# Operands asked for earlier and in smaller lots, a weight copy placed by product count, and the next image's norm spread over other steps, in a hand-ordered attention kernel

## The chip, the cores and the metric

The kernel runs on one core of a Trainium2 chip. The metric is device time in microseconds, the median of several runs. The core has the engines PE (TensorE, matmuls; PEld is its weight load), DVE (VectorE), ACT (ScalarE), POOL (GpSimd) and SP (SyncE, here only an issuer of DMAs).

## The reference

Two layers work on x, four images of 32 x 32 tokens with 768 channels, in float32. Each layer is a group norm (32 groups), an attention with 12 heads of 64 channels, decomposed relative positions in its scores, an output projection, and the addition to x.

```python
def attention(x, Wqkv, Wproj, Rh, Rw):             # x: (4, 32, 32, 768), normed
    q, k, v = split(x @ Wqkv)                      # 12 heads, S = 1024 tokens, 64 each
    bias = q . Rh (rows)[..., :, None] + q . Rw (columns)[..., None, :]
    attn = softmax(scale * q @ k.T + bias)         # 1024 x 1024 for each head
    return (attn @ v) @ Wproj                      # + bias of the projection

x = x + attention(group_norm(x), ...layer 0...)
x = x + attention(group_norm(x), ...layer 1...)    # with a bias on q, k and v
```

## The kernel before

**Pairs and steps.** Two layers of four images are eight passes, called images (`im`, 0 to 7). An image has six pairs of heads, so there are 48 pairs `g`; pair 0 of an image is the first, pair 5 the last. A pair takes eight steps `n`, of 128 query rows for both heads, 384 steps in all. The loop over `units` writes the order of the instructions of every engine by hand; nothing is reordered later. In a step it issues, among others, the position sums of two steps ahead (`biases`, L461 on POOL), the scores of the next step (`scores`: PE L475, DVE L484, ACT exp L488), a part of the work in `todo`, the transposes of this step (`turn`, DVE L515) and the division of the next (`divide`: DVE reciprocal L495, then POOL L499 for one head and ACT L501 for the other).

**The way of the probabilities.** DVE transposes 32 x 32 blocks into `tb`, two steps to a tile. At odd steps both tiles are written to DRAM (`td`, L518), and a few steps later read back in another order (`pt`, L526), for the product with v (`weigh`, PE L545; then the copy to `attn`, DVE L554 or L557). There are three `tb` buffers for two tiles in a quarter, so the second transpose of an even step waits until the last write of td has landed.

**Fill work.** `todo` is a list of generators: the projection of q and k of the next pair (`project_in`, PE L268), half a projection of v (`project_values`, PE L376, DVE L390 and L391), and four groups of the output projection (`project_out`, PE L621). `take(todo, n)` advances it by n products. `shares` says how many products a step takes, `first` how many of them are issued ahead of the transposes: in an ordinary pair [6, 9, 0, 6, 6, 6, 12, 0], the 12 in step 6 being the output groups.

**Projection of q and k.** Pairs 0 of each image and pair 1 are plain, with four units of six products. For the others, sums of weights and of inputs save three products: units of 6, 3, 6 and 6. (A pair g is called regular below when the pair after it, whose units it issues, is of this kind.) The sums of weights are made on POOL and ACT one pair earlier (`sum_weights`, L327 to L329), but for the last, which may only be made when unit 0 has read w0: DVE copies three blocks of w3 over the upper half of w0 (L336; the block A11 of the weights), POOL subtracts w3 from the lower half of w0 (L337). Unit 1 reads the copy, unit 2 what POOL wrote. Unit 0 is issued in step 0, units 1 and 2 in step 1. Then `positions` (PE L408, ACT L418) projects q on the position tables; its results go through DRAM (`tdr`) and come back as `rel` (SP L447).

**Output projection.** It is done in two parts p of three channel blocks each, with the partial sums kept in DRAM (`part`): part 0 of an image in its pairs 3 to 5, part 1 in the first three pairs of the next image. A group (o, i) has three matmuls of 128 x 512; then DVE adds the residual or the partial sum (L630 or L632) and the result is written back. `fetch` loads for four groups two tiles of weights (`wo`, pool of 2) and four of `res` (pool of 4, which the position tiles `t` and the tiles for the statistics of other images share), all in step 5, for groups in step 6.

**PSUM.** Of the tag "m" there are two buffers, which pj, pv, tp, av and o use in turn. So a fourth group needs that DVE is through with the second.

**DMA.** SP issues nearly all DMAs, in the order of the program. SP's and ACT's use eight semaphores in turn, so that an issue waits until the DMA eight places back has landed.

**The next image.** In pair 3 of an image the statistics of the next one are turned into means and scales (`stages`). In pair 4 its 12 tiles of x are loaded (`load_x`, three in each of steps 1 to 4) and normed in place (`apply`, DVE L228): tiles 0 and 1 in step 2, one in each of steps 3, 4 and 5, five in step 6, two in step 7.

The lists `early`, `later`, `mid`, `last`, `behind` and `behind2` hold issues that are put off: `early` runs at the start of a step, `later` becomes `early` in the next, `behind` runs after the scores.

## Time and profile before

| | us |
|---|---|
| median of 3 runs | 3700.49 (3692.12 to 3705.09) |
| profiled execution | 3706.17 |
| its span in the profile | 3704.4 |
| PE busy | 3465.2 (94%) |
| DVE busy | 2573.0 (69%) |
| POOL busy | 2495.1 (67%) |
| ACT busy | 1990.5 (54%) |
| matmuls of the projection of q and k (L268) | 958.5 |
| matmuls of the output projection (L621) | 509.1 |
| DVE norm applies (L228), 96 of | 0.536 each (median) |
| DMA | 1051.56 MB, 284 GB/s in the mean |

The mean granted clock of TensorE is 0.979 of the full one. A row of a group of instructions reads: line, engine, operation, output <- inputs with their shapes, count; then the busy time, the mean of one in ns, the time that the engine stood idle just before them, and what ended most of that. In the timeline, the number in brackets is the idleness of the engine ahead of the instruction and what ended it.

### The profile page before, as it was taken

To read this page: it belongs to the slowest core of one execution; us is meant where nothing else is said; L and a number is where in the kernel's file an instruction comes from. 1 tells how busy PE (TensorE), PEld (TensorE's weight loads), DVE (VectorE), ACT (ScalarE), POOL (GpSimd) and SP (SyncE) were. 2 spreads that over 40 slices of the span, in tenths; PEclk is the share of its full clock that TensorE was granted. 3 is DMA by queue.
4 is the path that set the end of the run, shared out by engine and by line. 5 is a ranking of instruction groups with operands and counts; after the bars stand their busy time and mean duration, and the time that the engine had idled before them with its cause. 6 is when DMAs were issued, how large, how long until landed. Compare 5 with 4: busy or idle time off the path is not lost.

```text
span 3704.4 us, 56289 instructions
## 1 busy us (share of the span) xinstructions
PE 3465.2 (94%) x20652; PEld 1942.2 (52%) x20652; DVE 2573.0 (69%) x4011; ACT 1990.5 (54%) x3958; POOL 2495.1 (67%) x1510
## 2 busy tenths in 40 slices
PE   6899999998999999999999999999999999999999
PEld 3455555555555555555455555555555555555554
DVE  4677767767677676767677766766766677666766
ACT  3665555455554556545555555555655555555543
POOL 3867686665866668666686666866668666776663
PEclk9999999999999999999999999999999999999999
DMA  3788878788787887878887887788887888787878
GB/s 113 252 295 294 310 277 298 273 297 314 269 308 271 297 299 274 289 287 303 286 290 270 300 306 276 287 290 285 297 297 271 299 284 311 262 291 284 288 267 298
DMA packets 531222, 1051.56 MB, mean 284 GB/s; under 512 B 143873, under 2 KB 206849, under 8 KB 481793
## 3 DMA queue, kind: packets, MB, share of 16 engines
q1 hardware_dynamic: 476448, 1020.53, 77.1%
q10 hardware_dynamic: 54496, 27.43, 2.5%
q8 instruction: 162, 2.65, 0.3%
q14 instruction: 116, 0.94, 0.1%
HBM read 572.73 MB, written 475.10 MB: 283 GB/s over the span
## 4 chain that ended last, share of the span: by engine, by line
PE 36%; DMA 26%; DVE 14%; ACT 9%; issue 6%; POOL 5%; SPq 4%; ACTq 0%; DVEq 0%; POOLq 0%
DMA td<-tb 16%; PE o L621 12%; PE pj L268 10%; DVE tb L515 7%; PE av L545 6%; DMA wo<-in_wo 6%; PE s L475 6%; DVE sc L484 4%; POOL sc L461 3%; SPq L447 3%; ACT rel L431 2%; ACT sc L488 2%; ACT sc L501 2%; PE tp L408 2%; PE pv L376 1%
## 5 line engine op out<-in xcount | busy, mean ns | idle before, releaser
L461 POOL TENSOR_TENSOR sc<-rel,rel 128x1024 f32<-128x1024 f32 x768 | 1543.1, 2078 | 43.6 <-DMA rel<-tdr 36.8
L488 ACT ACTIVATE sc<-sc,sm 128x1024 f32<-128x1024 f32 x768 | 879.6, 1146 | 743.5 <-DVE sm L484 740.5
L499 POOL TENSOR_SCALAR sc<-sc,sm 128x1024 f32<-128x1024 f32 x384 | 444.3, 1157 | 1057.2 <-DVE sm L495 1028.4
L484 DVE CUSTOM_DVE_ANT_0 sc<-s,sc 128x1024 f32<-128x1024 f32 x768 | 909.0, 1221 | 222.6 <-PE s L475 145.4
L268 PE MATMUL pj<-x,w 64*128 64x512 f32 x4140 | 958.5, 606 | 106.0 <-DVE w L336 66.9
L515 DVE STREAM_TRANSPOSE tb<-sc 128x1024 f32<-128x1024 f32 x768 | 916.8, 1225 | 153.1 <-DMA td<-tb 152.5
L501 ACT ACTIVATE sc<-sc,sm 128x1024 f32<-128x1024 f32 x384 | 440.9, 1148 | 625.9 <-DVE sm L495 625.9
L268 PEld LDWEIGHTS pj<-x,w 64*128 64x128 f32 x4140 | 452.3, 192 | 590.2 <-issue 387.7
L475 PE MATMUL s<-k,q 64*128 64x512 f32 x3072 | 754.0, 599 | 7.1 <-DVE sm L484 6.9
L545 PE MATMUL av<-pt,v 128*64 128x256 f32 x6144 | 696.7, 385 | 20.5 <-DVE q L243 18.9
L545 PEld LDWEIGHTS av<-pt,v 128*64 128x64 f32 x6144 | 439.7, 139 | 307.1 <-issue 63.6
L621 PE MATMUL o<-attn,wo 128*128 128x512 f32 x1080 | 509.1, 627 | 96.8 <-DMA wo<-in_wo 89.8
L376 PE MATMUL pv<-wv,x 64*128 64x256 f32 x4608 | 515.7, 377 | 1.2 <-DVE k L243 1.1
L376 PEld LDWEIGHTS pv<-wv,x 64*128 64x128 f32 x4608 | 449.1, 187 | 93.5 <-issue 33.4
L475 PEld LDWEIGHTS s<-k,q 64*128 64x128 f32 x3072 | 294.9, 187 | 297.7 <-issue 268.6
L621 PEld LDWEIGHTS o<-attn,wo 128*128 128x128 f32 x1080 | 210.0, 200 | 395.5 <-issue 244.7
L431 ACT COPY rel<-t 32x64 f32<-32x64 f32 x1504 | 363.3, 242 | 16.5
L346 POOL TENSOR_TENSOR x<-x,x 64x512 f32<-64x512 f32 x144 | 179.4, 1267 | 44.1 <-ACT x L348 28.9
L418 ACT COPY t<-tp 128x512 f32<-128x512 f32 x188 | 110.3, 586 | 163.2 <-PE tp L408 76.2
L243 DVE TENSOR_TENSOR k<-pj,k 128x512 f32<-128x512 f32 x173 | 117.5, 688 | 69.5 <-ACT k L291 26.3
L391 DVE TENSOR_TENSOR v<-pv,v 128x256 f32<-128x256 f32 x192 | 81.5, 424 | 110.7 <-ACT v L388 107.6
L488 ACT ACTIVATION_READ_ACCUMULATOR sc<-sc,sm 128x1 f32 x768 | 143.3, 187 | 0.0
(54 smaller groups left out, 1496.9 us busy)
## 6 DMA issues: line engine op xcount, KB each, us to landing
td<-tb SPq DMA_DIRECT2D x384, 1024.0 KB, 7.7
pt<-td SPq DMA_DIRECT2D x382, 1024.0 KB, 7.3
w<-in_wqk SPq DMA_DIRECT2D x96, 384.0 KB, 5.3
tdr<-t ACTq DMA_DIRECT2D x94, 256.0 KB, 4.9
x<-in_x SPq DMA_DIRECT2D x84, 256.0 KB, 7.6
part<-res SPq DMA_DIRECT2D x84, 256.0 KB, 2.0
res<-part SPq DMA_DIRECT2D x84, 256.0 KB, 8.9
wv<-in_wv SPq DMA_DIRECT2D x24, 768.0 KB, 9.9
```

The source lines that it names most:

```text
L268: nc.tensor.matmul(t[:, a, :], lhsT=w[a][rows, c, :], rhs=x[c][rows, :], start=(c == 0), stop=(c == len(x) - 1),)
L376: nc.tensor.matmul(t[:, a, k, :], lhsT=xs[i // 2 * NC + c][rows, at * P : (at + 1) * P], rhs=w[rows, c, :], start=(c == 0), stop=(c == NC ...
L431: nc.scalar.copy(rel[of, :, j, :], t[of, j, :, at : at + HW])
L461: nc.gpsimd.tensor_tensor(sc.rearrange("p (a k) (u l) -> p a l (k u)", a=4, l=8), rel0[:, h, :].unsqueeze(1).unsqueeze(2).to_broadcast(shape),
L475: nc.tensor.matmul(ps[h][:, cols], lhsT=q[rows, n * P : (n + 1) * P], rhs=k[rows, cols], start=True, stop=True,)
L484: nc.vector.tensor_tensor_reduce(out=sc, in0=ps[h], in1=sc, scale=-scale, scalar=BIG, op0=ALU.add, op1=ALU.min, accum_out=st[:, 0, h : h + 1],
L488: nc.scalar.activation(sc, sc, AF.Exp, bias=st[:, 0, h : h + 1], scale=-1.0, accum_out=st[:, 1, h : h + 1],)
L499: nc.gpsimd.tensor_scalar(sc, sc, st[:, 2, h : h + 1], 1.0, ALU.mult, ALU.mult)
L501: nc.scalar.activation(sc, sc, AF.Copy, scale=st[:, 2, h : h + 1])
L515: nc.vector.transpose(tb[:, :, j, :], sc_of[g, n, h])
L545: nc.tensor.matmul(av[rows, at * 2 * P : (at + 1) * 2 * P], lhsT=v_of[g][:, k, rows], rhs=pt_of[g, quarter, h][:, :, k, :], start=(k == 0) ...
L621: nc.tensor.matmul(t, lhsT=wo_of[im, o, c], rhs=attn_of[im * NP + c, i], start=(c == c0), stop=(c == c1 - 1),)
```

## The change

It has four parts.

1. The weights of the output projection, `wo`, are loaded by a function of their own, which is called in step 2 instead of step 5.
2. The four `res` tiles are loaded by twos, two in step 4 and two in step 5.
3. The copy over A11 is issued inside unit 0 of `project_in`, after its third product (c == 2), and in step 0 three products are issued ahead of the transposes (`first`). So on DVE it stands ahead of the two transposes of the step and the reciprocal. POOL's subtraction stays where it was.
4. In pair 4 the x tiles of the next image are loaded six in step 1, three in step 2 and three in step 4; the applies are three in step 2, one in each of steps 3, 4 and 5, four in step 6 and two in step 7.

On PE, ACT and POOL the order of the instructions is the same as before. On SP's queue the loads of wo now stand right behind the writes of td of step 1, ahead of those of w and pt; the first two of res stand behind the load of w and ahead of the reads of pt, the other two behind these reads and ahead of the writes of td of step 5, as all four did.

```diff
--- before.py
+++ after.py
@@ -269,6 +269,9 @@
                     t[:, a, :], lhsT=w[a][rows, c, :], rhs=x[c][rows, :],
                     start=(c == 0), stop=(c == len(x) - 1),
                 )
+            if c == 2 and unit == 0 and not plain(g):
+
+                nc.vector.tensor_copy(w0[TOP, :3], w3[LOW, :3])
             if c < len(x) - 1:
                 yield True
 
@@ -294,7 +297,7 @@
             add(to, t[1], to)
         elif unit == 0:
             nc.scalar.copy(k[0], t[0])
-            sum_weights_last(g)
+            nc.gpsimd.tensor_tensor(w0[LOW], w0[LOW], w3[LOW], ALU.subtract)
             add(q[0], u[1], k[0].rearrange("p a m -> p m a"), bias[0])
         elif unit == 1:
             add(k[0], t[0], k[0])
@@ -317,6 +320,9 @@
 
     def sum_weights(g):
 
+
+
+
         w0, w1 = w_of[g, 0], w_of[g, 1]
         w3 = w_of[g, 3] = wpool.tile([P, NC, P], FP, tag="w3", name=f"w_{g}_3")
 
@@ -329,12 +335,6 @@
             nc.gpsimd.tensor_tensor(w1[TOP], w0[TOP], w1[TOP], ALU.subtract)
 
         return first, second
-
-    def sum_weights_last(g):
-
-        w0, w3 = w_of[g, 0], w_of[g, 3]
-        nc.vector.tensor_copy(w0[TOP, :3], w3[LOW, :3])
-        nc.gpsimd.tensor_tensor(w0[LOW], w0[LOW], w3[LOW], ALU.subtract)
 
     def sum_input(im, n):
 
@@ -570,7 +570,7 @@
     part_of, res_of = {}, {}
     fetched = [0, 0]
 
-    def fetch(upto):
+    def fetch_weights(upto):
 
         while fetched[0] <= min(upto, len(parts) - 1):
             im, p, o, i = parts[fetched[0]]
@@ -586,6 +586,9 @@
                 for c in range(c0, c1):
                     wo_of[im, o, c] = w[:, c - c0, :]
             fetched[0] += 1
+
+    def fetch(upto):
+
         while fetched[1] <= min(upto, len(parts) - 1):
             im, p, o, i = parts[fetched[1]]
             l, b = images[im]
@@ -639,6 +642,7 @@
             nc.sync.dma_start(out=dst, in_=to)
         if i == 1 and (im, p, o, i) in place:
             if end and o > 1:
+                fetch_weights(place[im, p, o, i] + 4)
                 fetch(place[im, p, o, i] + 4)
         yield True
 
@@ -730,7 +734,7 @@
             if pair == 4 and not end:
                 if n == 0:
                     make_room(im + 1)
-                for c in range(3 * n - 3, 3 * n) if 1 <= n <= 4 else ():
+                for c in {1: range(NC), 2: range(6, 9), 4: range(9, NX)}.get(n, ()):
                     load_x(im + 1, c % NC, c // NC)
             if (im, pair) == (B - 1, 4) and n in (5, 7):
                 (load_table if n == 5 else scale_table)(1)
@@ -738,8 +742,9 @@
             early, later = later, early
 
             upto = 4 * (pair % 3) + 3
-            if n == 5 and (im, pair) >= (0, 3):
-                fetch(place[((im, 0) if pair >= 3 else (im - 1, 1)) + divmod(upto, 2)])
+            if n in (2, 4, 5) and (im, pair) >= (0, 3):
+                upto -= 2 if n == 4 else 0
+                (fetch_weights if n == 2 else fetch)(place[((im, 0) if pair >= 3 else (im - 1, 1)) + divmod(upto, 2)])
 
             ask = [divmod(g + 3, NP)] if n == 1 else []
             if im == 0 and pair < 3:
@@ -759,7 +764,7 @@
             if pair == 3 and n in stages and not end:
                 stages[n]()
             share = shares[n]
-            first = 3 if n == (6 if late else 7) else 2 if end and pair == NP - 1 and n in (3, 4) else 0
+            first = 3 if n == (6 if late else 7) or n == 0 and g + 1 < NPAIR and not plain(g + 1) else 2 if end and pair == NP - 1 and n in (3, 4) else 0
             first = min(first, share)
             take(todo, first)
             share -= first
@@ -767,7 +772,7 @@
             if at + 1 < len(units):
                 divide(*units[at + 1])
             if pair == 4 and not end:
-                for c in {2: (0, 1), 3: (2,), 4: (3,), 5: (4,), 6: range(5, 10), 7: (10, 11)}.get(n, ()):
+                for c in {2: (0, 1, 2), 3: (3,), 4: (4,), 5: (5,), 6: range(6, 10), 7: (10, 11)}.get(n, ()):
                     if n == 6 and c % 2 == 0:
                         take(todo, 3)
                         share -= 3
```

## The prediction

> **What bounds the kernel now.** I read the shares of busy time first, then the clock row, then the waits by line, and last the timelines of the two steps in which PE waits.

> ```profile
> PE 3465.2 (94%) x20652; PEld 1942.2 (52%) x20652; DVE 2573.0 (69%) x4011; ACT 1990.5 (54%) x3958; POOL 2495.1 (67%) x1510
> PEclk9999999999999999999999999999999999999999
> ```

> PE is busy for 94% of the span, and the clock is nearly whole. What can be won is in some 240 us of PE idleness. The waits view (us in all, times, longest) names the two that the change aims at and the one that I hold responsible:

> ```profile
> PE o L621 <- DMA wo<-in_wo: 89.8, 37, 6.1
> PE pj L268 <- DVE w L336: 66.9, 39, 7.2
> DVE tb L515 <- DMA td<-tb: 152.5, 67, 4.4
> ```

> Together the first two are 156.7 us, 4.2% of the span. The question is what is late next. Here is the timeline of pair 42 in steps 0 to 1 (PE, then DVE, then POOL; start, length, engine, line):

> ```profile
> 3256.91 8.29 PE L268 MATMUL pj<-x,w 64*128 64x512 f32 x36 [1.05 <-DVE w L336]
> 3265.35 1.16 PE L408 MATMUL tp<-tab,q 64*128 64x128 f32 x16
> ...
> 3255.18 1.25 DVE L515 STREAM_TRANSPOSE tb<-sc 128x1024 f32<-128x1024 f32 x1 [2.53 <-DMA td<-tb]
> 3256.35 0.12 DVE L495 RECIPROCAL sm<-sm 128x2 f32<-128x2 f32 x1
> 3256.50 0.35 DVE L336 COPY w<-w 64x384 f32<-64x384 f32 x1
> ...
> 3263.79 2.21 DVE L243 TENSOR_TENSOR k<-pj,k 128x512 f32<-128x512 f32 x3
> ...
> 3256.57 1.27 POOL L499 TENSOR_SCALAR sc<-sc,sm 128x1024 f32<-128x1024 f32 x1 [0.99 <-DVE sm L495]
> 3257.93 1.81 POOL L337 TENSOR_TENSOR w<-w,w 64x768 f32<-64x768 f32 x1
> ```

> The copy is late because the second transpose stands before it, and that waits 2.53 us for a DMA. But POOL's half of the same weight sum (L337) comes after L499, which waits for the reciprocal after the same transpose. And the same pair in step 6:

> ```profile
> 3299.80 7.99 PE L621 MATMUL o<-attn,wo 128*128 128x512 f32 x18 [1.03 <-DMA wo<-in_wo]
> 3308.70 2.84 PE L621 MATMUL o<-attn,wo 128*128 128x512 f32 x6 [0.91 <-DVE res L632]
> ...
> 3306.77 1.25 DVE L515 STREAM_TRANSPOSE tb<-sc 128x1024 f32<-128x1024 f32 x1 [2.25 <-DMA td<-tb]
> 3307.98 1.26 DVE L632 TENSOR_TENSOR res<-o,res 128x512 f32<-128x512 f32 x2
> ```

> Three of the four output groups run after the wait for wo; the fourth then waits again, for the PSUM buffer that L632 gives free, and L632 stands on DVE behind the second transpose, again held up by a DMA of td. Windows in step 6 of pair 8 (length, PE, PEld, DVE, ACT, POOL busy, granted clock, DMA share, GB/s) show how full DMA is there, and what a long wait costs besides:

> ```profile
> 714.00:718.40 4.40, 2.50 (x12) 0.96 (x9) 3.98 (x8) 3.09 (x4) 4.30 (x3) 1.00 1.05 389
> 718.40:721.80 3.40, 3.40 (x6) 1.34 (x5) 0.00 (x1) 1.28 (x4) 0.78 (x1) 0.50 1.06 420
> ```

> After about 2 us without a matmul, PE runs 3.40 us at half clock.

> [...] Here L336 takes 355 ns as a rule and up to 4087, and a norm apply (L228) 536 and up to 2273.

> **The change, part by part.**

> *The copy and unit 1.* No instruction is added; DVE's 39 copies move ahead of both transposes and the reciprocal, to the point where three products are done. There DVE is free (in pair 42 scores L484 end at about 3251.4), so in most pairs the copy takes 0.35 us and is hidden in the 2.53 us that the transpose waits. Unit 1 can then start 1.05 us earlier. It is 3 products of 9, so a third of 8.29 us, 2.76 us. Today PE comes to unit 2 at 3256.91 + 2.76 = 3259.67; L337, which unit 2 needs, ends at 3257.93 + 1.81 = 3259.74. So PE would arrive at 3258.62 and wait until 3259.74: 1.1 us of wait in a new place. The instructions of L337 on POOL keep their order, and the reciprocal ahead of them gets no earlier. Nor does tp, which needs the k adds of L243, at the end of the DVE chain that starts at that transpose. I take **0 us**, with bounds 0 to +67 won (the whole wait), and +5 lost: in the first pair of an image POOL is in a weight sum when the copy comes, and the copy may cost its up to 4 us, still about covered by the transpose's wait.

> *wo in step 2.* The two loads (192 KB each) go from step 5, between pt and td on SP's queue, to step 2, behind td and ahead of w and pt. They land after a median of 8.7 us, and are needed four steps later: o's first wait is gone. In their new place they delay w and pt by 384 KB at about 400 GB/s, 1 us; their readers come steps later. Two buffers suffice, since the groups that read the old ones are done by step 7 of the pair before.

> *res by twos.* Two of four loads (256 KB each) move to step 4, two stay in step 5, ahead of td. SP is busy with small rel loads from 3283.36 to 3289.6, so the first two get out hardly sooner than today. No gain and no cost, with 1 us either way if they get ahead of rel.

> *Step 6.* The ideal length is four groups of 2.6 us plus the scores, 12.3 to 12.5 us; the regular pairs take 13.4 to 17.7. The gain is not the wait for wo but what td gains: 384 KB fewer in front of it, at 389 to 420 GB/s, **0.9 to 1.0 us**. In pairs 0 and 2 of an image (some 13 regular ones) this arrives at PE, together 12; three of them also regain a clock window of half of 3.4 us, 1.7 each, 5. Pair 1 of an image is bound by DVE (v adds that wait for ACT: DVE L391 waits 107.6 us in all), I take 4 for the seven. Pair 3 has the norm's statistics on DVE, 0. In pair 4, DMA also brings the next image's x; td_5 comes late anyway and 4 to 6 us of idleness move from the first group to the fourth, with the half clock again: 0. Sum **21 us won** (bounds 0 and 45).

> *The norm of the next image, pair 4, seven times.* Six x loads instead of three go out in step 1, ahead of td; the same number in all, each queue's later share is smaller. One of the applies moves from each of steps 3, 4, 5 and 6 to the step before, so step 2 has three instead of two. There DVE's attn copy, which frees the PSUM of unit 3, comes behind the applies; in pairs 4, 10 and 40 PE already waits for it by 1.4 to 1.9 us, in the others it has 0.1 to 1.2 us to spare. The third apply costs 0.54 us, or up to 2.27 [...], and POOL is in L461 there. Seven times that, less the slack of about 3 in all: 1 to 13 us lost. ACT's block on DMA slots in this step ends sooner by a few us in all, since td's landing has other predecessors: 0 to 5 won. One apply fewer in step 6 wins DVE time only. I take **9 lost** (bounds 16 lost, 5 won).

> The sum is 0 + 21 - 9 = 12 won. The profiled execution took 3706.17 us (span 3704.4), so 3694.2 for it. It stands 5.7 above the median of the three, 3700.49; on the median's footing this is **3688**. A measurement of this kernel tells about 0.3%, 11 us, from no change.

> **The rivals.**

> *B: both waits really go.* For it: they are the largest that PE has, and halves of clock windows follow them. Against it: the timelines show the second releaser within 0.1 us of unit 2, and 0.91 us of a second wait in step 6. If two thirds of 156.7 us are won, and some ten clock windows by 1.7: 104 + 17, about 3580; if only the wo part is, about 3635. I put it at 3580 to 3665.

> *C: nothing arrives.* The chain td, transpose, reciprocal sets both steps; td gains nothing because DMA serves pt and res first just as late. Speaks for it: td waits of 152.5 us, and DMA at 400 GB/s throughout step 6. Then 3695 to 3706.

> *D: slower.* One mechanism: in pair 4 the third apply in step 2 [...] (2.27 us), the attn copy and unit 3 follow, and PE's wait of now 1.9 us grows to 4[...]: 2.2 + 1.7 = 3.9 us, seven times 27, while step 6 wins only about 10. Then 3717. It decides once more than about 3 us per pair 4 are lost. For it: gaps of 1.9 and 1.75 us are there already.

> **How the numbers follow.** The case forecast, 0.44 (3676 to 3700; three quarters of it beyond 0.3%); B 0.20; C 0.10; D 0.26, a tenth of it within 0.3%. Faster: 0.33 + 0.20 = 0.53. Same: 0.11 + 0.10 + 0.02 = 0.23. Slower: 0.24. The range leaves out the far half of B and the end of D: 3640 to 3718; the likeliest case alone is 3676 to 3700.

> **What would show it.** Right: the waits of L621 for wo and of L268 for L336 gone from the list; in their place L268 waiting for POOL's L337 with some 40 to 60 us, L621 for res adds with more than today's 30; tb's wait for td shorter by 20 to 40 us. In pair 4, an L228 of about 2 us in step 2 and a longer wait before unit 3. Wrong: L337 ending before PE has done unit 1, so that step 1 is shorter by 1 us in each pair, which is B; or td landing as late as today, which is C; or new half-clock windows in steps 2 and 3, which is D.

## The result, and the profile after

The changed kernel takes **3719.57 us** in the median (3718.02 to 3728.82, 6 runs), the kernel before 3701.2 (3688.1 to 3707.29, 6 runs): 1.006 times as long, 95% interval 1.0039 to 1.0081. Faster, 3688, had been forecast, with 3640 to 3718 as the range.

Two lines of the page of the kernel after, the same as were shown of the kernel before:

```profile
PE 3469.1 (93%) x20652; PEld 1944.2 (52%) x20652; DVE 2619.6 (70%) x4011; ACT 1990.2 (54%) x3958; POOL 2489.6 (67%) x1510
PEclk9999999999999999999999999999999999999999
```

PE, ACT and POOL are as busy as before, to within 6 us. DVE is busy for 46.6 us more with the same 4011 instructions: the 39 copies take 30.8 us more in sum, the 96 norm applies 14.0. The waits view of the kernel after (us in all, times, longest):

```profile
DVE tb L515 <- DMA td<-tb: 182.5, 69, 6.0
...
PE pj L268 <- DVE q L245: 31.9, 20, 2.9
...
PE o L624 <- DVE res L635: 29.1, 21, 3.4
PE o L624 <- DVE res L633: 28.3, 8, 5.6
...
PE pj L268 <- DVE q L243: 27.1, 20, 2.6
```

The same two kinds of wait in the kernel before:

```profile
PE o L621 <- DVE res L632: 3.0, 5, 0.9
PE pj L268 <- DVE q L243: 0.5, 1, 0.5
```

The two waits that the change aims at are gone from the head of the list: 66.9 us of L268 for the copy (10.9 are left) and 89.8 us of L621 (now L624) for wo. In their place L268 waits for DVE's q add, 31.9 + 27.1 = 59.0 us, and the output groups for res adds, 57.4 us. So most of the two waits has changed its name. (The prediction's "today's 30" for the res adds is the 18.0 + 12.0 us of the view of the tile wo, which counts PE's weight loads too.)

The transposes wait longer for td than before, 182.5 us for 152.5. By steps, the idleness of DVE ahead of the second transpose falls from 131.6 to 92.2 us in step 0, where the copy now stands in the wait, and grows from 16.4 to 80.3 in step 6. Yet that transpose does not start later in step 6: 9.6 us after the step's begin in the median of the pairs 3 to 46, where it was 10.1. DVE had waited for the late output groups first (res adds for PE, 86.3 + 74.5 us, now 38.4 + 41.7), and now comes to the wait for td sooner.

Cutting both timelines where the scores of the next step begin gives the length of every step. Summed over the 47 pairs g = 0 to 46, after less before:

| step | 0 | 1 | 2 | 3 | 4 | 5 | 6 | 7 | sum |
|---|---|---|---|---|---|---|---|---|---|
| us | -3.9 | +13.8 | -7.9 | +14.9 | +5.6 | +3.6 | -14.6 | +0.4 | +11.9 |

The spans differ by 12.9 us (3717.3 and 3704.4). Step 1 and step 3 lose more than step 6 wins. In step 1, 10.2 us are lost in the seven pairs 0 of images 1 to 7 and 9.7 in pairs 1 to 3 of the program; all the other pairs together win 6.0. The loss in step 3 is all in pairs 4 of the images. Such sums come from one execution of each kernel. Two kernels below, whose step 6 is as before outside the pairs 4 (the copy alone and the norm alone), differ there from the kernel before by -4.1 and +8.9 us, so some us in step 6 can't be told from none.

Pair 6, the first pair of the second image, shows where step 1 is lost. Its timeline, DVE and then POOL (start, length, engine, line), first of the kernel before:

```profile
517.16 1.24 DVE L515 STREAM_TRANSPOSE tb<-sc 128x1024 f32<-128x1024 f32 x1
521.20 1.25 DVE L515 STREAM_TRANSPOSE tb<-sc 128x1024 f32<-128x1024 f32 x1 [2.79 <-DMA td<-tb]
...
517.35 3.98 POOL L461 TENSOR_TENSOR sc<-rel,rel 128x1024 f32<-128x1024 f32 x2
```

Then of the kernel after:

```profile
522.87 4.10 DVE L274 COPY w<-w 64x384 f32<-64x384 f32 x1 [0.17 <-POOL w L335]
527.00 2.37 DVE L515 STREAM_TRANSPOSE tb<-sc 128x1024 f32<-128x1024 f32 x2
...
522.78 3.98 POOL L461 TENSOR_TENSOR sc<-rel,rel 128x1024 f32<-128x1024 f32 x2
```

The copy starts 0.09 us after POOL's first L461 and ends 0.2 us after POOL's second (522.78 + 3.98 = 526.76; 522.87 + 4.10 = 526.97). It lasts 4.10 us where it takes 0.36 in most pairs. Only then do both transposes come, one after the other without a wait for td: they are late because of the copy, not of a DMA. The meeting is no accident. The copy waits for POOL's weight sum L335 (0.17 us), and L461 is what POOL does next. All seven pairs 0 show it, with 4.09 to 4.11 us. In pair 1 the copy first waits 5.29 us for L335; in pairs 1 to 3 it then takes 4.09, 3.83 and 3.84 us beside two L461, where it took 4.09, 1.54 and 1.54 behind the transposes.

Step 6 of pair 42 in the kernel after, PE and then DVE (the prediction has the same step of the kernel before):

```profile
3309.76 7.99 PE L624 MATMUL o<-attn,wo 128*128 128x512 f32 x18
3320.20 4.54 PE L624 MATMUL o<-attn,wo 128*128 128x512 f32 x6 [2.44 <-DVE res L635]
...
3318.26 1.25 DVE L515 STREAM_TRANSPOSE tb<-sc 128x1024 f32<-128x1024 f32 x1 [3.78 <-DMA td<-tb]
3319.43 0.12 DVE L495 RECIPROCAL sm<-sm 128x2 f32<-128x2 f32 x1
3319.47 1.26 DVE L635 TENSOR_TENSOR res<-o,res 128x512 f32<-128x512 f32 x2
```

Three groups now start without a wait. The fourth waits 2.44 us, where it waited 0.91, and then takes 4.54 us, where it took 2.84. What is behind the wait is the first DVE line: a transpose that waits for td. What is behind the longer run is the clock, in the window from the start of that group (length, PE, PEld, DVE, ACT, POOL busy, granted clock, DMA share, GB/s):

```profile
3320.20:3323.60 3.40, 3.40 (x5) 1.49 (x6) 0.54 (x1) 0.54 (x1) 3.32 (x3) 0.56 0.58 226
```

In this pair the idleness, gathered in one place, is followed by a stretch at little over half clock too, 0.56; in the same place before (3308.70 to 3312.10) it was 1.00. Over the whole span it is the other way: the time at half clock falls from 154.9 us to 118.9. Nor is the prediction's "about 2 us" without a matmul a sharp limit. In the trace before, a half-clock stretch begins during the wait or within 3.5 us behind it for 2 of the 40 waits of PE of 1.0 to 1.9 us, for 6 of 14 of 1.9 to 2.2 us, and for 30 of 35 longer ones.

### The profile page after: what moved, and what is told of

Its sections match the earlier page's. It is cut to its first block, busy times and chain, and to the rows that moved or that the text cites. A ratio compares the mean times of both kernels' runs of the same rounds, so it can differ in the third digit from the quotient of the medians.

```text
span 3717.3 us, 56361 instructions
## 1 busy us (share of the span) xinstructions
PE 3469.1 (93%) x20652; PEld 1944.2 (52%) x20652; DVE 2619.6 (70%) x4011; ACT 1990.2 (54%) x3958; POOL 2489.6 (67%) x1510
## 4 chain that ended last, share of the span: by engine, by line
PE 29%; DVE 23%; DMA 19%; ACT 15%; issue 8%; POOL 6%; SPq 0%; ACTq 0%; DVEq 0%; POOLq 0%
DMA td<-tb 17%; DVE tb L515 9%; DVE sc L484 7%; PE s L475 7%; PE o L624 7%; PE av L545 6%; PE pj L268 5%; ACT rel L431 4%; ACT sc L488 4%; ACT sc L501 4%; PE pv L376 3%; POOL sc L461 2%; PE tp L408 2%; DVE k L243 1%; DVE w L274 1%
## 5 line engine op out<-in xcount | busy, mean ns | idle before, releaser
L461 POOL TENSOR_TENSOR sc<-rel,rel 128x1024 f32<-128x1024 f32 x768 | 1545.1, 2081 | 42.5 <-DMA rel<-tdr 35.6
L499 POOL TENSOR_SCALAR sc<-sc,sm 128x1024 f32<-128x1024 f32 x384 | 436.7, 1137 | 1076.3 <-DVE sm L495 977.4
L268 PE MATMUL pj<-x,w 64*128 64x512 f32 x4140 | 971.0, 607 | 123.1 <-DVE q L245 31.9
L484 DVE CUSTOM_DVE_ANT_0 sc<-s,sc 128x1024 f32<-128x1024 f32 x768 | 909.4, 1222 | 221.8 <-PE s L475 146.9
L515 DVE STREAM_TRANSPOSE tb<-sc 128x1024 f32<-128x1024 f32 x768 | 917.6, 1226 | 183.8 <-DMA td<-tb 182.5
L268 PEld LDWEIGHTS pj<-x,w 64*128 64x128 f32 x4140 | 458.5, 192 | 609.2 <-issue 406.9
L545 PE MATMUL av<-pt,v 128*64 128x256 f32 x6144 | 690.8, 383 | 21.7 <-DVE q L243 19.0
L545 PEld LDWEIGHTS av<-pt,v 128*64 128x64 f32 x6144 | 435.8, 138 | 306.2 <-issue 50.5
L624 PE MATMUL o<-attn,wo 128*128 128x512 f32 x1080 | 514.7, 625 | 78.4 <-DVE res L635 29.1
L624 PEld LDWEIGHTS o<-attn,wo 128*128 128x128 f32 x1080 | 203.4, 197 | 382.1 <-issue 254.9
L243 DVE TENSOR_TENSOR k<-pj,k 128x512 f32<-128x512 f32 x173 | 117.7, 689 | 64.8 <-ACT k L294 26.2
L391 DVE TENSOR_TENSOR v<-pv,v 128x256 f32<-128x256 f32 x192 | 81.5, 424 | 111.5 <-ACT v L388 108.4
## 6 DMA issues: line engine op xcount, KB each, us to landing
wv<-in_wv SPq DMA_DIRECT2D x24, 768.0 KB, 13.4
```

The costliest lines, as they stand in the source:

```text
L268: nc.tensor.matmul(t[:, a, :], lhsT=w[a][rows, c, :], rhs=x[c][rows, :], start=(c == 0), stop=(c == len(x) - 1),)
L461: nc.gpsimd.tensor_tensor(sc.rearrange("p (a k) (u l) -> p a l (k u)", a=4, l=8), rel0[:, h, :].unsqueeze(1).unsqueeze(2).to_broadcast(shape),
L484: nc.vector.tensor_tensor_reduce(out=sc, in0=ps[h], in1=sc, scale=-scale, scalar=BIG, op0=ALU.add, op1=ALU.min, accum_out=st[:, 0, h : h + 1],
L499: nc.gpsimd.tensor_scalar(sc, sc, st[:, 2, h : h + 1], 1.0, ALU.mult, ALU.mult)
L515: nc.vector.transpose(tb[:, :, j, :], sc_of[g, n, h])
L545: nc.tensor.matmul(av[rows, at * 2 * P : (at + 1) * 2 * P], lhsT=v_of[g][:, k, rows], rhs=pt_of[g, quarter, h][:, :, k, :], start=(k == 0) ...
```

## The experiments

The kernel before was timed beside each of them on the same chip; its median lay between 3704.6 and 3708.7 us there. Read the ratios, with their intervals (95%).

**The copy alone.** In the kernel before:

```diff
+            if c == 2 and unit == 0 and not plain(g):
+                nc.vector.tensor_copy(w0[TOP, :3], w3[LOW, :3])
-            sum_weights_last(g)
+            nc.gpsimd.tensor_tensor(w0[LOW], w0[LOW], w3[LOW], ALU.subtract)
...
-            first = 3 if n == (6 if late else 7) else ...
+            first = 3 if n == (6 if late else 7) or n == 0 and g + 1 < NPAIR and not plain(g + 1) else ...
```

> The kernel before with the third part of the change alone: the copy over A11 after three products, ahead of the transposes. Theory ([...] in the first pair of each image, so the copy takes 4.1 us instead of 0.35 and both transposes come later; in pairs 1 to 3 it also waits in DVE's queue for POOL's sums): step 1 longer by 1.4 to 2.3 us in the seven pairs 0 and by 2 to 5 us in pairs 1 to 3, all others the same within 0.5 us on average; 12 to 20 us slower in all, about 3715. Rival (the early wo loads lengthen step 1, since td lands later): the same as before, 3700, within 4. Rival (the copy's wait of 66.9 us is really won): 3640 to 3660.

Measured: 3721.25 us, ratio 1.0046 (1.0029 to 1.0063). Step 1 is 21.4 us longer in sum: 12.2 in the pairs 0, 9.8 in pairs 1 to 3 of the program, -0.6 in all others. This part is enough to account for most of the loss of the whole change, and in a regular pair, where POOL is not in L461, it wins nothing.

**The same copy on ACT** in just these pairs, everything else as in the changed kernel:

```diff
-                nc.vector.tensor_copy(w0[TOP, :3], w3[LOW, :3])
+                (nc.vector.tensor_copy if (g - 1) % NP and g > 4 else nc.scalar.copy)(w0[TOP, :3], w3[LOW, :3])
```

> The changed kernel, but in the first pair of each image and in pairs 1 to 3 ACT makes the early copy instead of DVE. Theory [...]: the copy takes below 0.7 us there, the transposes in pairs 0 start where they do in other pairs, step 1 of pairs 0 is shorter by about 10 us in sum than in the changed kernel; 10 to 17 us faster than the changed kernel, about 3705. Rival ([...] the place in the program costs, whichever engine copies): the same as the changed kernel, 3719, within 4.

Measured: 3690.86 us, ratio 0.9967 (0.9957 to 0.9978); the changed kernel had 1.006. Pair 6 of this kernel, ACT and then DVE:

```profile
512.64 0.51 ACT L274 COPY w<-w 64x384 f32<-64x384 f32 x1
...
511.26 1.24 DVE L515 STREAM_TRANSPOSE tb<-sc 128x1024 f32<-128x1024 f32 x1
515.35 1.25 DVE L515 STREAM_TRANSPOSE tb<-sc 128x1024 f32<-128x1024 f32 x1 [2.85 <-DMA td<-tb]
```

At the same place in the program, with POOL in the same L461, the copy takes 0.51 us, the first transpose follows the scores at once, and the second waits for td as it did before the change. The pairs 0 lose 1.4 us in step 1 instead of 10.2, pairs 1 to 3 win 3.7 instead of losing 9.7. It is DVE's copy beside POOL that costs, not the place. The gain on the changed kernel, some 29 us, is about twice what was expected. Of 28 us between the two traces 21 are in step 1, more of them in pairs 1 to 3 (13.4) than in the pairs 0 (8.8), and 4.7 in step 6.

**The change without the early copy** (the copy again on DVE behind the reciprocal, the rest of the change as it is):

```diff
-            if c == 2 and unit == 0 and not plain(g):
-                nc.vector.tensor_copy(w0[TOP, :3], w3[LOW, :3])
...
+            nc.vector.tensor_copy(w0[TOP, :3], w3[LOW, :3])
             nc.gpsimd.tensor_tensor(w0[LOW], w0[LOW], w3[LOW], ALU.subtract)
```

> The changed kernel without its third part: the copy on DVE behind the reciprocal, as before; wo, res, loads and applies as in the changed kernel. Theory (all the loss is the early copy's, in pairs 0 to 3 of the program and the first pair of each image; elsewhere the early copy wins nothing, since unit 2 and tp wait for the same transpose): the same as the version with the copy on ACT, 3691, within 5. Rival (an early copy [...] does win about 1 us in each regular pair): 3705 to 3725. Rival (the parts don't add): anything near the changed kernel's 3719.

Measured: 3698.52 us, ratio 0.9984 (0.9974 to 0.9994), 7 us more than expected. So wo, res and the norm together win about 6 us. The version with the copy on ACT has the lower ratio, but the intervals touch; whether an early copy that doesn't meet POOL wins something is left open. Nor do the parts quite add: the copy alone (1.0046) and all the rest (0.9984) make 1.003, the whole change has 1.006, at the edge of what the intervals allow.

**wo and res alone**, in the kernel before: `fetch_weights` in step 2, `fetch` by twos in steps 4 and 5, as in the change's diff; copy, loads and applies as before.

> The kernel before with the first two parts alone: wo in step 2, res by twos. Theory (the first output group's wait for wo goes, but the fourth group waits for a res add behind the second transpose, which waits for td): step 6 shorter by 12 to 25 us in sum over all pairs, of 90 us of wait for wo; 15 to 25 us faster in all, about 3681. Rival (what the first group wins the fourth loses wholly): 3697 to 3703. Rival (full gain, and the other parts eat it): 3610 to 3640.

Measured: 3703.32 us, ratio 0.9999 (0.9986 to 1.0012). The rival was right on the time: a gain of 15 to 25 us is excluded. In the trace step 6 is 1.1 us longer in sum, and the waits of the output groups for res adds are 36.9 + 30.8 = 67.7 us, in place of 89.8 for wo. A loss comes with it, in step 3 of the pairs 4, 6.7 us; the applies there start 1.5 us later in the mean. ACT's waits in this kernel name the likely cause:

```profile
ACT t L416 <- DMA wo<-in_wo: 27.0, 4, 7.0
ACT v L386 <- DVE v L389: 26.8, 50, 0.8
ACT t L416 <- DMA x<-in_x: 22.1, 5, 8.5
```

ACT's second copy of position results stands behind its own DMA issue, and that waits for a slot among the eight: now for a wo load behind x loads. In the kernel before, ACT's position copies wait for no wo.

**The norm alone**, in the kernel before:

```diff
-                for c in range(3 * n - 3, 3 * n) if 1 <= n <= 4 else ():
+                for c in {1: range(NC), 2: range(6, 9), 4: range(9, NX)}.get(n, ()):
...
-                for c in {2: (0, 1), 3: (2,), 4: (3,), 5: (4,), 6: range(5, 10), 7: (10, 11)}.get(n, ()):
+                for c in {2: (0, 1, 2), 3: (3,), 4: (4,), 5: (5,), 6: range(6, 10), 7: (10, 11)}.get(n, ()):
```

> The kernel before with the fourth part alone: six x loads in step 1 of pair 4 and three applies in step 2. Theory (the third apply takes 2.25 us [...] and delays the attn copy that unit 3 waits for): step 3 of the seven pairs 4 longer by 10 to 16 us in sum, pair 5 in sum the same; 8 to 16 us slower, about 3712. Rival (the loads, not the apply, decide: td and tdr behind six x loads): step 2 longer, step 3 only by what step 2 is late. Rival (it's the fetch that moved the step): the same as before, 3700.

Measured: 3701.05 us, ratio 0.999 (0.9977 to 1.0003), no difference that can be told. The third apply does take 2.26 to 2.28 us in each pair 4. But ACT gets its slot earlier (its position copies wait 21.0 us for td and x, where it was 42.6), and the applies start 0.8 to 3.7 us earlier in step 2, 2.4 in the mean. That covers the 2.2 us by which the third apply puts off the attn copy: step 3 of the pairs 4 is 4.7 us shorter in sum, not longer. The expectation fell.

**wo late in pair 4 only**, the copy on ACT where POOL runs:

```diff
+                if n == (5 if pair == 4 else 2):
+                    fetch_weights(to)
+                if n > 2:
+                    fetch(to)
```

> The version of the change with the copy on ACT in the first pairs, but in pair 4 of each image wo is loaded in step 5 as before. Theory (in pair 4 the two wo loads of step 2, behind six x loads, hold the DMA slots that ACT's position write waits for, so that ACT, the three applies and the attn copy come late): step 3 of pairs 4, in sum 13 us longer than in the kernel before with wo in step 2, is 3 to 7 us shorter than there; step 6 of pairs 4 gets the wait for wo back, some 5 to 14 us. In all 3 to 15 us faster than with wo in step 2, about 3683. Rival (the third apply [...] costs by itself): step 3 stays 8 us longer or more, 3690 to 3700.

Measured: 3716.47 us, ratio 1.0018 (1.0007 to 1.0029). Step 3 of the pairs 4 is 4.7 us shorter than before the change, where it is 13.0 longer with wo in step 2. The third apply is the same in both (2.27 and 2.25 us), and from the start of the applies to the end of the attn copy it takes 2.2 us more than before in both. What differs is the start: 2.4 us earlier than before with wo in step 5, 0.3 with wo in step 2. So the third apply costs step 3 only where wo in step 2 takes away the earlier start that hides it. But step 6 of the pairs 4 takes 36 us more than with wo in step 2 (L624 waits 55.7 us for wo, in 8 places). The forecast of the total was wrong by 33 us; why wo comes so late there is not shown.

**td ahead of pt**, in the kernel before and with nothing of the change. The writes of td of steps 5 and 7 had the reads of pt of steps 4 and 7 ahead of them on SP's queue; in pairs 3 to 46 these reads are put off by two steps and by one:

```diff
-                (behind if quarter % 2 else behind2).append(
+                step = NT * g + n + ((2, 3, 3, 1) if 2 < g < NPAIR - 1 else (2, 1, 2, 1))[quarter]
+                due.setdefault(step, []).append(
                     lambda queue=None, h=h, td=td: read_back(g, quarter, h, td, queue)
                 )
...
-            run(behind)
-            behind, behind2 = behind2, behind
+            run(due.pop(at, []))
```

> The kernel before, nothing of the change, but in pairs 3 to 46 the reads of pt of steps 4 and 7 are issued two steps and one step later, so that the writes of td of steps 5 and 7 stand ahead of them in SP's queue. Theory (the second transposes of steps 0 and 6 wait for td because 2 MB of pt are in front of it): DVE's waits of L515 for td, 152 us, fall below 60; L336's wait of 66.9 us goes too, though the copy hasn't moved; step 6 still waits for wo, somewhat longer or shorter. 40 to 70 us faster, about 3650. Rival (td is held up by bandwidth, whatever stands in front): waits stay, 3695 to 3710. Rival (pt comes too late for the product with v in steps 7 and 2): new waits of L545 for pt, 3710 to 3760.

Measured: **3494.98 us, ratio 0.9442 (0.9421 to 0.9463)**, a gain of some 210 us where 40 to 70 were expected. Its page begins

```profile
span 3491.0 us, 56390 instructions
...
PE 3395.4 (97%) x20652; PEld 1897.0 (54%) x20652; DVE 2576.5 (74%) x4011; ACT 1990.4 (57%) x3958; POOL 2496.7 (72%) x1510
```

and its waits have

```profile
PE o L622 <- DVE v L391: 16.7, 15, 2.0
...
DVE tb L515 <- DMA td<-tb: 13.0, 11, 1.7
...
PE pj L268 <- DVE w L336: 9.1, 3, 6.1
```

The transposes' wait falls from 152.5 to 13.0 us, PE's wait for the copy from 66.9 to 9.1, though the copy stands where it stood, and the wait for wo is gone too, though wo is still loaded in step 5: it no longer stands behind 2 MB of pt, and lands after a median of 3.6 us instead of 8.7. Step 6 of pair 42 in this kernel, PE and DVE:

```profile
3107.30 10.57 PE L622 MATMUL o<-attn,wo 128*128 128x512 f32 x24
...
3110.79 2.36 DVE L515 STREAM_TRANSPOSE tb<-sc 128x1024 f32<-128x1024 f32 x2
```

Four groups in one piece. By steps, the sum over the pairs is -97.5 us in step 1, -32.5 in step 2, -87.5 in step 6. PE is busy for 70 us less with the same matmuls. The time at half clock falls from 154.9 to 40.7 us, and half of that difference, 57 us, is my estimate of its share. Over the whole program the product with v waits 1.2 us for pt: there was that much room.

**Only one of the two reads put off**, that of step 7 (`(2, 1, 3, 1)` in the line above):

> Only the read of pt of step 7 goes behind the write of td, that of step 4 stays as before. Theory (each step's wait is set by its own td): step 1 is shorter by 95 us in sum over the pairs 3 to 46 and step 2 of the pairs 5 by some 30, as with both; step 6 stays within 25 us of the kernel before; about 3575 to 3600. Rival (the gain of step 6 follows from step 1 being early): step 6 is shorter by 60 us or more, below 3540.

Measured: 3584.75 us, ratio 0.9657 (0.9642 to 0.9672), as expected. Step 1 is 94.7 us shorter, step 2 32.5, step 6 2.7 longer. So each step hangs on its own write: step 1 on that of step 7, step 6 on that of step 5. Here wo, again behind the read of step 4, lands after 8.6 us.

**td ahead of pt, with wo in step 2 and res by twos:**

> The same order of td ahead of pt, with the first two parts of the change (wo in step 2, res by twos) in the kernel before. Theory: with td early, the fourth output group no longer waits for the res add, so that now the wait for wo, once removed, is won: another 40 to 70 us, about 3595. Rival (step 6 is then bound by DVE and ACT): 3630 to 3650, no better than td ahead of pt alone by more than 20.

Measured: 3500.99 us, ratio 0.9455 (0.9435 to 0.9474). It wins nothing more. The theory, by which the removed wait for wo would now be worth another 40 to 70 us, falls: td ahead of pt had freed wo already.

**td ahead of pt, with the whole change** and the copy on ACT in the first pairs:

> The whole change with the copy on ACT in the first pairs, and td ahead of pt. Theory: as with the first two parts and td ahead, and here the early copy makes no difference, since the reciprocal is early too: about 3590. Rival (the norm's six loads in step 1 or the early copy gain once td is not the bound): below 3575.

Measured: 3502.5 us, ratio 0.9459 (0.9439 to 0.9478). The change as a whole wins nothing here either.

**td ahead of pt, with the norm alone:**

> td ahead of pt, with the fourth part (x loads and applies) alone. Theory: as in the kernel before, the loads by six win some 5 us in pairs 4, in step 3: 3485 to 3493. Rival (with td early pairs 4 have no slack left in step 3 and the third apply costs): 3497 to 3510. Rival (nothing): 3495 within 3.

Measured: 3496.1 us, ratio 0.942 (0.9405 to 0.9435); in medians 1 us from td ahead of pt alone, as the second rival had it. The third part of the change was not tried here by itself. The smallest edit is as good as any that was tried, and beats both kernels by over 5%.

## Why the prediction was wrong

**The copy: the step that failed.** The prediction took 0 us and bounded the loss at 5, "still about covered by the transpose's wait". Alone, the copy costs 17 us by the medians (21.4 in step 1 by its trace). What happens was named nearly rightly: in the first pair of an image POOL is busy and the copy takes up to 4 us, though what it meets is L461 and not the weight sum. Two things were mis-sized.

First, the wait does not cover the copy. The prediction's own figures say so: 4.09 us less the wait of 2.53 leaves 1.56 a pair, 11 us in seven pairs. Before the change the second transposes of step 0 of the pairs 0 waited 2.5 to 4.1 us for td; with the change they wait for nothing, behind a copy of 4.1 us. In pair 6 the pair's step 0 starts at 518.20 and the second transpose ends at 527.00 + 2.37 = 529.37, 11.17 later; in the kernel before, at 512.76 and 521.20 + 1.25 = 522.45, 9.69 later. These 1.5 us are also what step 1 of the pairs 0 is longer by on average (10.2 in seven).

Second, the pairs 1 to 3 of the program, where the copy meets L461 as well and in pair 1 also waits for POOL's sum, were not looked at; they lose 9.7. The trace before has the copy at 1.5 to 4.09 us in just these.

What holds DVE's copy up beside POOL is not shown. The traces have the times: 4.10 us for the copy, which in pair 6 ends 0.2 us after the second of two POOL instructions, and 0.51 for the same copy on ACT.

**The copy: the step that held.** In the other pairs the early copy wins nothing, as worked out: -0.6 us over all of them. The releaser is another than was named, DVE's q add, which frees the PSUM buffer that unit 2 needs, and not POOL's L337; POOL's result comes some 0.4 us later (in pair 6 of the kernel after L300, its L337, ends at 532.52, the q add at 532.15). Both hang on the reciprocal behind the same transpose, so the number stood. The 6.0 us that these pairs win in the whole change are not the copy's: with wo and res alone they win 6.1.

**Step 6.** 21 us were taken, 14.6 were found in the whole change, and none (1.1 lost) with wo and res alone. The mechanism is the one described: the wait goes from the first group to the fourth, behind the res add, the transpose and td. But that the sum came near it is in part luck. From pair 3 on, the terms were 17 won in the pairs 0 and 2 and 4 in the pairs 1; found were, each give or take some us, 1.0 in the pairs 0 and 2 together, 6.1 in the pairs 1, and 5.7 in the pairs 4, which stood at nothing. The term that was mis-sized is the author's estimate for td, 0.9 to 1.0 us for 384 KB fewer in front of it: the second transpose starts 0.5 us sooner in the median, 0.3 with wo and res alone, since 2 MB of pt still stood ahead of td. With these behind td, that transpose starts 7.3 us after the step's begin, not 9.6. The sign for tb's wait, 20 to 40 us shorter, was wrong too: it is 30 longer, for DVE comes to it sooner. Rival C, for which nothing arrives in step 6, was right for wo and res alone, within what one trace can tell.

**The norm.** 9 us lost were taken, at most 16, for the third apply beside POOL. In the changed kernel step 3 of the pairs 4 loses 14.9 us, by the mechanism named: the third apply takes 2.25 us, and with it the attn copy ends 2.2 us later, seven times. But alone the part loses nothing. Two terms were mis-sized, and in the changed kernel they nearly cancel. ACT's earlier slot, taken as 0 to 5 us won in all, lets the applies start 2.4 us earlier in each pair 4. The two wo loads of step 2, taken at nothing since "their readers come steps later", make them start 1.5 us later when alone, and with the six x loads they undo the earlier start (0.0 in the mean). That they do it by the DMA slots that ACT waits for is what ACT's waits suggest (for td, x and wo together 42.6 us before, 21.0 with the norm alone, 46.8 in the changed kernel); it was not tested apart. The prediction looked at the readers of what the loads delay, not at the slots that they hold.

**The rivals.** D, slower, had the right sign and part of the cause. In the pairs 4 and 40 PE's wait before unit 3 grows from 1.9 and 1.4 us to 4.0, as it said, but step 3 loses 14.9 us of the 27 that it named, with one half-clock stretch more in steps 2 and 3 of these pairs, not seven. The larger loss, the copy's, was not in it, so that its 3717 lies near the measured time is luck. B, two thirds of the waits won by the change, fell. But that the waits could be won together was true: by moving what stands ahead of td, not what waits behind it. The prediction had the chain in its own fences (L515 waits for td in both timelines) and never asked what stands in front of td on SP's queue besides wo.

## What to carry to other kernels

When a wait has a second releaser close behind, don't move the first: follow both back to where they meet, here a DMA write, and ask what is ahead of it in its queue (here 2 MB of pt: with these behind the write, the wait for it fell from 152.5 us to 13.0). Before an instruction is moved ahead of others on its engine, look at every pair or stage in which its new neighbours on other engines differ, and cost it with its longest time in the trace, less the wait that it really fills. A load moved to a quiet place need not be free: with wo and res alone, ACT's position copies waited 27.0 us for wo; in the kernel before they waited for none.

## What the runs showed of the hardware that was not expected

```profile
1747.91 3.98 DVE L228 TENSOR_SCALAR x<-x,nrm 128x512 f32<-128x512 f32 x3
...
1749.39 4.41 POOL L461 TENSOR_TENSOR sc<-rel,rel 128x1024 f32<-128x1024 f32 x2
```

The third apply takes 2.27 us and ends at 1751.89, while POOL is at work until 1753.80; POOL's two take 4.41 us instead of 3.98. Why the copy ends behind both and the apply behind one is left open.
- Reads of pt ahead of a write of td, of 1 MB, held it up by some 6 us here. With those of steps 4 and 7 moved behind the writes, the second write of td of step 7 lands a median of 6.5 us after its issue instead of 12.5. Over all writes of td it is 6.2 instead of 7.7, while pt takes 10.2 instead of 7.3, and the kernel is 5.6% faster.
